# Moving the mask's count, the scales' signs and a block's statistics between engines in an attention and feed-forward kernel

## The chip, the cores and the metric

The kernel runs on one core of a Trainium2 chip. The metric is the device time of one execution in microseconds (us). The core's engines work side by side, each through its own list of instructions, in order: TensorE (PE in the profile; PEld are its weight loads), VectorE (DVE), ScalarE (ACT), GpSimd (POOL) and SyncE (SP), which here only issues transfers. An engine waits on another only through semaphores.

## The reference

`x` has 2048 rows of 256 numbers and `ctx` 1601 rows of 192. The result is `x` plus a cross attention, plus a feed-forward net with three weight matrices of signs. Cut to what matters here:

```python
n = layer_norm(layernorm(x)) ; q = n @ Wq ; k, v = split(ctx @ Wkv)      # 16 heads of 64
k = concat([null_k, k]) ; v = concat([null_v, v])                        # one null key: 1602 keys
sim = where(pad(mask, True), (q * 64**-.25) @ (k * 64**-.25).T, -max)    # mask: 1601 flags
x = x + layer_norm(softmax(sim) @ v @ Wout)
h = concat([n, -n]), n = layernorm(x)
h = relu(s0 * h @ W0) * 2 ; h = relu(s1 * h @ W1) * 2 ; h = s2 * h @ W2  # W = +1 or -1
x = x + h
```

`s0`, `s1` and `s2` are single numbers read from memory.

## The kernel before

**Units.** Heads go in pairs, 8 of them, and rows of `x` in blocks of 512, 4 of them. The main loop runs over 32 units (pair p, block b), unit u = 4p + b. In a unit, 13 tiles of 128 keys pass through scores (L414, `sT`), exponential (L440, `e`) and the weighted sum with the values (L447, `av`). Beside the scores TensorE computes the next unit's row maxima (L373, read by VectorE in L376). The tail of a unit combines the maxima (L381), turns them by a transpose (L386) and spreads them (L388, `mT`, read from the PSUM tile `mt`), projects the unit before out (L460), projects the queries of the unit after next (L215) and a half of the next pair's keys (L247, L252) or values (L316, L328).

**Order.** Everything stands in a hand-written order (`manual_schedule`): each engine issues its instructions as the code writes them, and a framework only adds the waits that the data needs.

**The denominators.** GpSimd adds the 13 exponentials into `acc`: tiles 1 and 2 (L689), 3 to 7 (L691), and then tile 0 and tiles 8 to 12 (L699). Tile 0 holds the last 66 keys, and before L699 may add it, and before TensorE may use it (it is the last group of L447), ScalarE scales its rows 64 and up by the column `spent` (L697). In the next unit ScalarE copies one number out of the finished `acc` (L680, `seen`) ahead of its exponential of tile 2, and so stands still there until the sums of the unit before are done.

**The mask's count.** Masked keys are set equal to the null key, and their number has to be taken out again. `masked_counted` (unit 0) reduces the mask's flags on VectorE (L400), subtracts 1601 (L401), puts the result in one row with a column of the identity (L402) and adds two more such columns (L404): the column `spent`.

**Input statistics.** Blocks 2 and 3 of `x` are normalised in units 0 and 1: `input_root` takes statistics on VectorE (L79, L80) and the root on ScalarE (L508, which loads a function table), `input_normed` takes a reciprocal (L512) and the negated mean (L142) on VectorE and eight row operations on ScalarE (L145, L146); then a one-number exponential (L712) loads ScalarE's other table again. `input_turned` in the tail of the same unit transposes the block (L525) and scales it into `xnT` (L526, L530), which the query projection L215 reads. In unit 1 the statistics already follow L381 on VectorE.

**The scales' signs.** In unit 3 VectorE computes `sgn` (sign of s0 and s1) and `s_out` (8 |s0| |s1| s2) from `s_sb` in five operations (L748 to L752), behind the masking of the second half of `ctx_b` (L407) and ahead of L388. `sgn` is first read in unit 28, `s_out` in the last layer.

**What lies on both sides of it.** GpSimd also does `keys_stepped` (L272) once for each pair. SyncE's transfers in this part (`ctx_b` a second time, the next pair's weights) are issued ahead of time.

Of the kernel before, what the change touches and what calls it, by code (L numbers as in the profile page):

```python
# [12 lines left out]
AF = mybir.ActivationFunctionType  # L13
ALU = mybir.AluOpType
# [5 lines left out]
M = 1601  # L20
# [8 lines left out]
KLAST = KEYS - 128 * (KC - 1)  # L29
# [9 lines left out]
def xattn_ffn(ctx, tc, x, ctxT, mask, g_norm, null_kv, wq, wkv, wout, g_out, k0, k1, k2, s0, s1, s2, out):  # L39
    nc = tc.nc  # L40
# [17 lines left out]
    s_sb = cp.tile([128, 3], F32, name="s_sb")  # L58
    sgn = cp.tile([128, 2], F32, name="sgn")
    s_out = cp.tile([128, 1], F32, name="s_out")  # L60
    eps_sb = cp.tile([128, 1], F32, name="eps_sb")
    eps2_sb = cp.tile([128, 1], F32, name="eps2_sb")
    ident = cp.tile([128, 128], F32, name="ident")
# [6 lines left out]
    warm = cp.tile([128, 1], F32, name="warm")  # L70

    def stats(src, n, name, mv=None):

        at = 0 if mv is None else 2
        if mv is None:
            mv = sp.tile([128, 4, 2], F32, tag="mv", name=f"mv_{name}")
        for j in range(n):
            st = sp.tile([128, 6], F32, tag="st", name=f"st_{name}_{at + j}")
            nc.vector.bn_stats(st, src[:, j, :])  # L79
            nc.vector.bn_aggr(mv[:, at + j, :], st)  # L80
        return mv
# [8 lines left out]
    def centred(dst, src, mv, r, j):  # L90
        nc.vector.tensor_scalar(dst, src, mv[:, j, 0:1], r[:, j : j + 1], ALU.subtract, ALU.mult)  # L91
# [47 lines left out]
    def centred_beside(dst, src, mv, r, b):  # L139

        nm = sp.tile([128, 4], F32, tag="nm", name=f"nm_{b}_{n_slots}")
        nc.vector.tensor_scalar(nm, mv[:, :, 0], -1.0, None, ALU.mult)  # L142
        for j in range(4):
            t = 4 * b + j
            nc.scalar.activation(dst[:, t, :], src[:, t, :], AF.Identity, bias=nm[:, j : j + 1])  # L145
            nc.scalar.mul(dst[:, t, :], dst[:, t, :], r[:, j : j + 1])  # L146

    with ExitStack() as att:
# [15 lines left out]
        spent = ap.tile([128, 1], F32, name="spent")  # L164
# [213 lines left out]
        def max_combined(p, b):  # L378

            cols = mcol.rearrange("p (j c) -> p c j", j=2)[:, 0:4, :]  # L380
            nc.vector.tensor_reduce(cols, maxima[p, b], AX.X, ALU.max, negate=True)  # L381
# [16 lines left out]
        def masked_counted():  # L398

            nc.vector.tensor_reduce(spent, keep[:, 1:], AX.X, ALU.add)  # L400
            nc.vector.tensor_scalar(spent, spent, float(M), None, ALU.subtract)  # L401
            nc.vector.tensor_tensor(spent, spent, ident[:, KLAST : KLAST + 1], ALU.mult)  # L402
            for row in range(64, KLAST):
                nc.vector.tensor_tensor(spent, spent, ident[:, row : row + 1], ALU.add)  # L404

        def context_masked(part, start, end):
            nc.vector.tensor_tensor(part[:, start:end], part[:, start:end], keep[:, start:end], ALU.mult)  # L407
# [97 lines left out]
        def input_root(b):  # L505
            mv = stats(x_sb[:, ts(b, 4), :], 4, f"x{b}")
            r = sp.tile([128, 4], F32, tag="rstd", name=f"rstd_x{b}")
            nc.scalar.activation(r, mv[:, :, 1], AF.Sqrt, bias=eps2_sb, scale=1.0 + EPS)  # L508
            return mv, r

        def input_normed(b, mv, r, beside=False):
            nc.vector.reciprocal(r, r)  # L512
            if beside:
                centred_beside(y_sb, x_sb, mv, r, b)
                return
            for j in range(4):
                centred(y_sb[:, 4 * b + j, :], x_sb[:, 4 * b + j, :], mv, r, j)
# [131 lines left out]
        with tc.manual_schedule():  # L649
            for u, (p, b) in enumerate(units):  # L650
# [40 lines left out]
                        nc.gpsimd.tensor_tensor(acc, acc, es[k], ALU.add)  # L691
                if nxt is not None:
                    max_combined(*nxt)
                if u == 0:
                    masked_counted()

# [7 lines left out]
                if u == len(units) - 2:  # L704
# [2 lines left out]
                    norm_end(0, y_sb, y_sb, beside=True)  # L707

                    nc.scalar.activation(warm, eps_sb, AF.Exp)
                if u < 2:  # L710
                    input_normed(u + 2, *input_root(u + 2), beside=True)
                    nc.scalar.activation(warm, eps_sb, AF.Exp)  # L712
                if u == 0:


                    nc.sync.dma_start(out=ctx_b[64:, 1:KEYS], in_=ctxT[128:CD, :])


# [24 lines left out]
                    context_masked(ctx_b, 0, 1024)  # L743
                if u == 3:
                    context_masked(ctx_b, 1024, KEYS)


                    nc.vector.tensor_scalar(sgn, s_sb[:, 0:2], 0.0, None, ALU.is_ge)  # L748
                    nc.vector.tensor_scalar(sgn, sgn, 2.0, -1.0, ALU.mult, ALU.add)
                    nc.vector.tensor_tensor(s_sb[:, 0:2], s_sb[:, 0:2], sgn, ALU.mult)  # L750
                    nc.vector.tensor_scalar(s_out, s_sb[:, 0:1], s_sb[:, 1:2], 8.0, ALU.mult, ALU.mult)
                    nc.vector.tensor_tensor(s_out, s_out, s_sb[:, 2:3], ALU.mult)  # L752
                if p + 1 < NP and b in (1, 2):
                    round_k(p + 1, b - 1)
                avs = lp.tile([128, 512], F32, tag="avs", name=f"avs_{p}_{b}", bufs=1)
# [172 lines left out]
```

## Time and profile before

| what | value |
|---|---|
| time, median of 3 runs | 1285.53 us (1283.4, 1285.53, 1285.76) |
| the profiled execution's own time | 1286.19 us |
| its span | 1284.4 us, granted TensorE clock 0.994 on average |
| unit 0: exponentials start | 38.65 us |
| unit 3: sums on GpSimd (L699) | start 162.32, take 15.27 us |
| unit 7: the same | start 300.59, take 14.90 us |
| feed-forward part | from 1098.69 us on |

The span is the profiled execution from its first to its last instruction; its own time has some 1.8 us more around it. "Busy" is the time in which an engine has an instruction in work. A line of the timeline gives the start, the time taken, the engine, the line of the kernel, the operation with output and input, and how long the engine had been idle before, with what released it. A line of a table by windows gives, for one stretch, the busy time of TensorE, its weight loads, VectorE, ScalarE and GpSimd with the number of instructions, then the granted TensorE clock (1.00 is full speed), and what the transfers did. The chain of work that ended last is followed back from the last instruction to whatever released each step.

### The profile page before, as it was taken

To read this page: it belongs to the slowest core of one execution; us is meant where nothing else is said; L and a number is where in the kernel's file an instruction comes from. 1 tells how busy PE (TensorE), PEld (TensorE's weight loads), DVE (VectorE), ACT (ScalarE), POOL (GpSimd) and SP (SyncE) were. 2 spreads that over 40 slices of the span, in tenths; PEclk is the share of its full clock that TensorE was granted. 3 is DMA by queue.
4 is the path that set the end of the run, shared out by engine and by line. 5 is a ranking of instruction groups with operands and counts; after the bars stand their busy time and mean duration, and the time that the engine had idled before them with its cause. 6 is when DMAs were issued, how large, how long until landed. Compare 5 with 4: busy or idle time off the path is not lost.

```text
span 1284.4 us, 19605 instructions
## 1 busy us (share of the span) xinstructions
PE 1264.9 (98%) x8336; PEld 651.5 (51%) x8336; DVE 768.3 (60%) x831; ACT 716.8 (56%) x974; POOL 1005.9 (78%) x505
## 2 busy tenths in 40 slices
PE   8999989999999999999999999999999999999998
PEld 6334444444444444444444444444444433788887
DVE  6778676656665666565666566656666783644432
ACT  3676645666566656666666666666666666422120
POOL 5688978899889988999889988998899999801100
PEclk9999989999999999999999999999999999999999
DMA  5100000000000000000000000000000010000000
GB/s 145 23 1 5 1 1 13 5 1 1 14 5 1 1 14 5 1 1 14 5 1 1 1 13 5 1 1 5 1 17 1 1 42 1 1 12 6 17 17 17
DMA packets 16169, 13.40 MB, mean 10 GB/s; under 512 B 2689, under 2 KB 15553, under 8 KB 16081
## 3 DMA queue, kind: packets, MB, share of 16 engines
q1 hardware_dynamic: 14944, 11.02, 3.1%
q8 instruction: 65, 1.06, 0.3%
q10 hardware_dynamic: 656, 0.79, 0.2%
q0 software_dynamic: 480, 0.34, 0.2%
q14 instruction: 24, 0.19, 0.0%
HBM read 10.04 MB, written 2.10 MB: 9 GB/s over the span
## 4 chain that ended last, share of the span: by engine, by line
PE 87%; POOL 7%; DVE 2%; ACT 2%; DMA 1%; issue 1%; SPq 0%; DVEq 0%; POOLq 0%; ACTq 0%
PE sT L414 26%; PE av L447 23%; PE ps L810 11%; PE max L373 6%; PE po L460 4%; PE psq L215 4%; POOL acc L699 4%; POOL acc L691 3%; PE ps L841 2%; PE psv L316 2%; PE psk L247 2%; PE psv L328 1%; PE sT L438 1%; PE den L471 1%; PE psk L252 1%; DMA x_sb<-in_x 1%
## 5 line engine op out<-in xcount | busy, mean ns | idle before, releaser
L376 DVE TENSOR_REDUCE mx<-max 128x2 f32<-128x1024 f32 x384 | 444.0, 1219 | 90.2 <-PE max L373 86.4
L699 POOL TENSOR_TENSOR acc<-acc,e 128x1024 f32<-128x1024 f32 x192 | 473.3, 2465 | 16.8 <-ACT e L697 1.8
L440 ACT ACTIVATE e<-sT 128x1024 f32<-128x1024 f32 x416 | 424.9, 1023 | 88.0 <-PE sT L438 45.3
L414 PE MATMUL sT<-qT,kT 64*128 64x512 f32 x1664 | 445.0, 609 | 5.1 <-ACT e L440 5.0
L691 POOL TENSOR_TENSOR acc<-acc,e 128x1024 f32<-128x1024 f32 x160 | 378.9, 2368 | 12.5
L447 PE MATMUL av<-e,v 128*32 128x512 f32 x3328 | 363.6, 592 | 0.0
L373 PE MATMUL max<-kr,qr 64*128 64x512 f32 x768 | 280.8, 719 | 0.8 <-DVE mx L376 0.8
L447 PEld LDWEIGHTS av<-e,v 128*32 128x32 f32 x3328 | 107.6, 110 | 237.5 <-issue 229.9
L414 PEld LDWEIGHTS sT<-qT,kT 64*128 64x128 f32 x1664 | 134.6, 186 | 135.8 <-ACT e L440 123.5
L689 POOL TENSOR_TENSOR acc<-e,e 128x1024 f32<-128x1024 f32 x32 | 75.6, 2361 | 76.5 <-ACT e L440 76.5
L373 PEld LDWEIGHTS max<-kr,qr 64*128 64x128 f32 x768 | 76.7, 188 | 88.9 <-DVE mx L376 66.2
L489 ACT COPY aoT<-r 32x256 f32<-32x256 f32 x224 | 90.2, 403 | 33.5 <-DVE r L483 31.2
L756 ACT COPY avs<-av 128x512 f32<-128x512 f32 x32 | 18.7, 585 | 145.0 <-PE av L447 145.0
L388 DVE TENSOR_TENSOR mT<-mt,pick 128x512 fp32r<-128x512 f32 x32 | 22.1, 691 | 116.9 <-PE mt L386 116.9
L490 DVE TENSOR_TENSOR aoT<-avs,aoT 128x512 f32<-128x512 f32 x28 | 26.9, 961 | 94.3 <-ACT aoT L489 94.3
L810 PE MATMUL ps<-h0hi,w 128*128 128x512 f32 x256 | 79.5, 392 | 0.0
L810 PE MATMUL ps<-h0lo,w 128*128 128x512 f32 x256 | 78.9, 390 | 0.0
L124 POOL TENSOR_TENSOR y_sb<-y_sb,gout_sb 128x256 f32<-128x256 f32 x12 | 9.3, 776 | 86.0 <-DVE y_sb L91 86.0
L216 ACT ACTIVATE qr<-psq 128x512 fp32r<-128x512 f32 x32 | 19.1, 597 | 95.0 <-PE psq L215 92.3
L798 ACT ACTIVATE h1hi<-ps 128x1024 fp32r<-128x1024 f32 x16 | 16.4, 1027 | 98.9 <-PE ps L810 98.9
L215 PE MATMUL psq<-xnT,wq 128*128 128x512 f32 x124 | 59.0, 599 | 2.0 <-ACT xnT L526 2.0
L460 PE MATMUL po<-wo,aoT 128*128 128x256 f32 x256 | 60.6, 380 | 0.0
(170 smaller groups left out, 1199.4 us busy)
## 6 DMA issues: line engine op xcount, KB each, us to landing
out_x<-o SPq DMA_DIRECT2D x7, 256.0 KB, 2.1
x_sb<-in_x SPq DMA_DIRECT2D x3, 512.0 KB, 9.1
wa<-in_wkv SPq DMA_DIRECT2D x8, 128.0 KB, 3.0
wq<-in_wq SPq DMA_DIRECT2D x8, 128.0 KB, 2.2
wo<-in_wout SPq DMA_DIRECT2D x8, 128.0 KB, 2.1
xnT<-in_k SPq DMA_DIRECT2D x1, 1024.0 KB, 5.5
wb<-in_wkv SPq DMA_DIRECT2D x15, 64.0 KB, 2.5
ctx_a<-in_ctxT SPq DMA_DIRECT2D x2, 256.0 KB, 7.3
```

The costliest lines, as they stand in the source:

```text
L215: nc.tensor.matmul(ps[:, 0, :], weights[p][0][:, c, :], xnT[:, b, c, :], start=c == 0, stop=c == 1)
L373: nc.tensor.matmul(ps[:, j, :w], qr[rows, ts(t, 128)], kr[rows, ds(start, w)], start=True, stop=True)
L376: nc.vector.tensor_reduce(maxima[p, b][:, t, :, c], ps[:, :, :w], AX.X, ALU.max)
L414: nc.tensor.matmul(ps[:n, j, :], kT[rows, ds(128 * KEY_TILES[k], n)], qT[rows, :], start=k < 2, stop=k >= 2, skip_group_check=k >= 2,)
L440: nc.scalar.activation(e, ps, AF.Exp)
L447: nc.tensor.matmul(av[ts(i, 32), 0, :], v[:n, KEY_TILES[k], ts(i, 32)], e[:n, i // 2, :], start=k == 1, stop=k == 0, tile_position=(0, 32 ...
L460: nc.tensor.matmul(pv[:, t, :], aoT[:, ts(t, 128)], weights[p][3], start=True, stop=True)
L489: nc.scalar.copy(aoT[ds(64 * j + 32 * rows, 32), ts(h, 256)], r[ds(64 * j + 32 * h, 32), :])
L689: nc.gpsimd.tensor_tensor(acc, es[1], es[2], ALU.add)
L691: nc.gpsimd.tensor_tensor(acc, acc, es[k], ALU.add)
L699: nc.gpsimd.tensor_tensor(acc, acc, es[k], ALU.add)
L810: nc.tensor.matmul(ps[:, f, :], w(c)[:, ts(2 * g + f, 128)], parts[part][:, c, :], start=i == 0, stop=i == len(steps) - 1,)
```

## The change

Three things are edited. In `masked_counted` the reduction of the mask stays on VectorE, and the small operations behind it go to GpSimd, the first two as one. The block that normalises blocks 2 and 3 of `x` (with its exponential of one number) is written ahead of the count and of the scaling by `spent`, instead of behind the sums of L699. The five operations on the scales go from VectorE in unit 3 to GpSimd in unit 4.

```diff
         def masked_counted():
 
             nc.vector.tensor_reduce(spent, keep[:, 1:], AX.X, ALU.add)
-            nc.vector.tensor_scalar(spent, spent, float(M), None, ALU.subtract)
-            nc.vector.tensor_tensor(spent, spent, ident[:, KLAST : KLAST + 1], ALU.mult)
+            nc.gpsimd.tensor_scalar(spent, spent, float(M), ident[:, KLAST : KLAST + 1], ALU.subtract, ALU.mult)
             for row in range(64, KLAST):
-                nc.vector.tensor_tensor(spent, spent, ident[:, row : row + 1], ALU.add)
+                nc.gpsimd.tensor_tensor(spent, spent, ident[:, row : row + 1], ALU.add)
...
                 if nxt is not None:
                     max_combined(*nxt)
+                if u < 2:
+                    input_normed(u + 2, *input_root(u + 2), beside=True)
+                    nc.scalar.activation(warm, eps_sb, AF.Exp)
                 if u == 0:
                     masked_counted()
 
                 nc.scalar.mul(es[0][64:], es[0][64:], spent[64:, 0:1])
                 for k in (0, *range(8, KC)):
                     nc.gpsimd.tensor_tensor(acc, acc, es[k], ALU.add)
...
-                if u < 2:
-                    input_normed(u + 2, *input_root(u + 2), beside=True)
-                    nc.scalar.activation(warm, eps_sb, AF.Exp)
                 if u == 0:
                     nc.sync.dma_start(out=ctx_b[64:, 1:KEYS], in_=ctxT[128:CD, :])
...
                 if u == 3:
                     context_masked(ctx_b, 1024, KEYS)
-                    nc.vector.tensor_scalar(sgn, s_sb[:, 0:2], 0.0, None, ALU.is_ge)
-                    nc.vector.tensor_scalar(sgn, sgn, 2.0, -1.0, ALU.mult, ALU.add)
-                    nc.vector.tensor_tensor(s_sb[:, 0:2], s_sb[:, 0:2], sgn, ALU.mult)
-                    nc.vector.tensor_scalar(s_out, s_sb[:, 0:1], s_sb[:, 1:2], 8.0, ALU.mult, ALU.mult)
-                    nc.vector.tensor_tensor(s_out, s_out, s_sb[:, 2:3], ALU.mult)
+                if u == 4:
+                    nc.gpsimd.tensor_scalar(sgn, s_sb[:, 0:2], 0.0, None, ALU.is_ge)
+                    nc.gpsimd.tensor_scalar(sgn, sgn, 2.0, -1.0, ALU.mult, ALU.add)
+                    nc.gpsimd.tensor_tensor(s_sb[:, 0:2], s_sb[:, 0:2], sgn, ALU.mult)
+                    nc.gpsimd.tensor_scalar(s_out, s_sb[:, 0:1], s_sb[:, 1:2], 8.0, ALU.mult, ALU.mult)
+                    nc.gpsimd.tensor_tensor(s_out, s_out, s_sb[:, 2:3], ALU.mult)
```

On VectorE the order in unit 0 becomes L381, statistics, reciprocal, negated mean, L400; on ScalarE, in units 0 and 1, the table load, the root, the eight row operations, the second table load and the exponential of one number stand ahead of L697. TensorE's and SyncE's instructions keep their order.

## The prediction

> **What bounds the kernel now.** I read the page's busy shares first, then the chain of work that ended last, then the timelines of ScalarE (ACT) and GpSimd (POOL) around the moved work, and last the granted clock by windows. "Unit" is one pass of the main loop (pair p, query block b, numbered 0 to 31); times are us from the span's start.
>
> ```profile
> PE 1264.9 (98%) x8336; PEld 651.5 (51%) x8336; DVE 768.3 (60%) x831; ACT 716.8 (56%) x974; POOL 1005.9 (78%) x505
> ...
> PE 87%; POOL 7%; DVE 2%; ACT 2%; DMA 1%; issue 1%; SPq 0%; DVEq 0%; POOLq 0%; ACTq 0%
> ```
>
> TensorE bounds nearly everything, so only places where it stands still can be won, or be made. The chain, in order of time, shows two such places where the edited lines stand; this is the one in unit 3:
>
> ```profile
> 163.17 2.00 issue
> 165.17 2.93 DVE ctx_b L407
> 168.10 2.25 DVE sgn L748
> 170.58 2.20 DVE s_sb L750
> 173.05 2.13 DVE s_out L752
> 175.18 0.61 DVE mT L388
> 175.84 2.50 PE psv L316 x10
> ```
>
> Columns are start, length, what. Three operations on two numbers take over 2 us each: each ends where a GpSimd sum ends. They hold L388, which frees the PSUM tile that L316 writes: the list of waits gives TensorE 3.9 us there. The other place is unit 0; first ScalarE, then GpSimd (start, length, engine, line, operation, idle before it and its releaser):
>
> ```profile
> 52.40 1.02 ACT L440 ACTIVATE e<-sT 128x1024 f32<-128x1024 f32 x1 [0.28 <-PE sT L414]
> 57.20 1.15 ACT L697 ACTIVATE e<-e,spent 64x1024 f32<-64x1024 f32 x1 [3.78 <-DVE spent L404]
> 58.37 1.28 ACT L508 ACT_TABLE_LOAD   x1
> ...
> 76.70 0.17 ACT L680 COPY seen<-acc 1x1 f32<-1x1 f32 x1
> ...
> 98.09 0.84 ACT L266 CAST kr<-kT 128x802 fp32r<-128x802 f32 x1
> ...
> 111.15 0.17 ACT L680 COPY seen<-acc 1x1 f32<-1x1 f32 x1
> ```
>
> ```profile
> 58.49 14.54 POOL L699 TENSOR_TENSOR acc<-acc,e 128x1024 f32<-128x1024 f32 x6 [1.79 <-ACT e L697]
> 77.97 2.37 POOL L689 TENSOR_TENSOR acc<-e,e 128x1024 f32<-128x1024 f32 x1 [4.94 <-ACT e L440]
> 80.41 12.16 POOL L691 TENSOR_TENSOR acc<-acc,e 128x1024 f32<-128x1024 f32 x5
> 92.65 16.40 POOL L699 TENSOR_TENSOR acc<-acc,e 128x1024 f32<-128x1024 f32 x6
> ```
>
> The reader is to see the coupling: the six sums of L699 start only after L697, and L680 in the next unit lets ScalarE go past k = 2 only when they are done. Unit 0's sums end at 73.03, and L680 comes at 76.70 (3.7 to spare); unit 1's end at 109.05 against 111.15 (2.1 to spare). Where nothing is spare the wait is real: the list of waits has
>
> ```profile
> ACT seen L680 <- POOL acc L699: 4.0, 3, 2.1
> ```
>
> (total us, times, longest; units 29 to 31). The windows show the clock falling behind both idle places:
>
> ```profile
> 70.00:72.00 2.00, 2.00 (x5) 0.83 (x3) 0.00 (x0) 1.14 (x3) 1.92 (x2) 0.50 0.00 0
> ...
> 176.00:178.00 2.00, 2.00 (x10) 2.00 (x10) 0.91 (x1) 0.00 (x0) 1.59 (x1) 0.50 0.00 0
> ```
>
> **Part 1, the signs leave unit 3 (gain).** Five VectorE operations go (2.31, 0.17, 2.19, 0.21, 2.13). L388 can then run when L407 ends (168.10) and its transpose is done (168.49), and L316 follows the query projection (170.06, 1.72 long as in unit 2) at 171.78 instead of 175.84. The price of stall and slow clock together comes from unit 7, the same block of the next pair, which has neither: from the copy L756 to L680 it takes 307.10 to 316.31 = 9.21; unit 3 takes 168.30 to 184.26 = 15.96. Gain 6.75. Its cover is thin: unit 3's sums end at 177.59, 9.29 behind L756, while L680 is now wanted at 9.21; unit 7's sums took 14.90 where unit 3's took 15.27, so I take no loss (0 to 0.4).
>
> The five operations on GpSimd stand behind unit 4's sums, where GpSimd idles 3.10 us before unit 5's first sum. The nearest row, 128x4 on GpSimd (L589), took 0.21: five are 1.05, hidden. Bounds: 0.14 (L587, 128x13) to 1.20 (L794, 128x1024 with pointer scalars), so 0.7 to 6.0; at 6.0 unit 5's sums are 2.9 late, 1.8 of it spare at unit 6's L680: up to 1.1 lost. The first reader of sgn is in unit 28.
>
> **Part 2, statistics ahead of the count, in units 0 and 1.** The diff moves the block not only past the count but past L697, and for `u < 2`. On ScalarE two table loads, the root, eight row operations and the warm-up (12 instructions) now stand ahead of L697; nothing of it is a DMA and the DMA queues keep their order.
>
> Unit 0. VectorE starts the statistics at 53.99, where the count was; in unit 1 they took 89.94 to 92.16 = 2.22, and the first operation behind the warm-up (L266) came 5.93 after that. So L697 starts at 53.99 + 2.22 + 5.93 = 62.14 and ends 63.29; with the same 0.14 to follow, the sums start at 63.43 (4.9 later) and end at 77.97. The count itself (1.81 from about 56.9) ends near 58.7, and three small GpSimd operations (0.6; 0.4 to 3.6) have 3.4 us until L697 is reached: nothing, at worst 0.2. TensorE's last group of L447 waits 0.35 for L697, and behind L697 stand L756 and L526, which wait for L447 and the transposes anyway. Then: L447 ends 64.2, transposes 1.09, scaled copy 0.75, projection at 66.1 instead of 67.43, at full clock (L215 1.72 and L247 1.35 as at 103.84 and 105.56, instead of 2.60 and 2.43: 1.96 less): the first scores of unit 1 come at 70.0 instead of 73.2. All of that is thrown away: L680 would be wanted 3.4 later, at 73.4 (in unit 2 it came at 111.15, the first scores at 107.78), and the sums end at 77.97. From L680 to the next scores took 1.16 (1041.41 to 1042.57, where L680 was waiting): 79.16 against 78.05 before. Loss 1.1.
>
> Unit 1 (times without that shift). L697 leaves 89.46 for the place of L266, 98.09; it ends 99.24, the sums start at 99.38 instead of 92.65. They take 14.54 rather than 16.40, since VectorE's two-input operations of 96.05 and 97.97 (2.00 and 4.00, stretched by waiting for GpSimd) are over. End 113.9 against 111.15 wanted; next scores 115.1 against 112.50. Loss 2.6. L447's last group (100.1) is not held.
>
> **The new idle time and the clock.** In unit 2 the scores behind L680 started 4.72 after the first ones (107.78 to 112.50), so in unit 1 TensorE could go on at 74.75 and stands still until 79.16, 4.4 us; in unit 2 2.6. Rows: 2.03 of idle in unit 0 was followed by half clock and cost 1.96; 3.90 in unit 3 cost 6.75 - 4.06 = 2.7; about 1.8 in unit 30 cost none (clock 1.00 from 1040 to 1044). So unit 1 pays 1.0 to 2.7, I take 1.9; unit 2 lies between the 1.8 without and the 2.03 and 3.90 with: 0 to 1.96, I take 1.0.
>
> The Trainium skill (TensorE: Matmul & The Clock Gate, "Why this matters for your kernels") speaks against this change: it asks for no idle gaps over about 3 us between bursts, since one window of idle halves the clock. By that rule unit 1 would pay and unit 2 not, and the sum would end 1.0 lower; the row of unit 0, slowed after 2.03, contradicts the rule's length, and I keep the rows.
>
> **Sum.** +1.1 + 2.6 - 6.75 + 1.9 + 1.0 = -0.15. The profiled execution took 1286.19 (span 1284.4 and 1.8 around it), so 1286.0; it lies 0.66 above the median of the runs, 1285.53, and carried to that the forecast is 1285.4. From unit 4 on both kernels issue the same work, and the shift travels unchanged.
>
> **Rivals** (times on the median).
> - The stalls cost no clock. -3.05: 1282.5, faster. For it: the 1.8 idle of unit 30; against: both longer idle places were slowed. 0.12.
> - L680 does not bite: unit 0's 3.2 and unit 3's 6.75 are both won, 1275.6. For it: it idles in 3 of 31 places only; against: the three show it bites as soon as the sums are late. 0.08.
> - GpSimd becomes the bound in units 3 and 4 (slower). With its sums 2.8 later and TensorE 6.75 earlier, unit 3's sums end after L680 is wanted. Decides from 9.21 us behind L756; before it was 9.29. If VectorE's two-input work stretches them as in unit 1 (16.40 for 14.90), ScalarE waits 1.5 in unit 4 and TensorE may pay a slow stretch of 1.96: -0.15 + 3.5, 1288.9. For it: the margin; against: unit 7. 0.25.
>
> **Chances.** The forecast has 0.55. 0.2% of the time, 2.6 us, is about what can be told from no change. Faster 0.20 (the first two rivals), same 0.55, slower 0.25 (the third). The unknowns make 1282.5 (no clock loss) to 1288.2 (-3.05 with 2.7, 1.96 and 1.1 for slow GpSimd operations on it) for the forecast; I reach up to 1288.9 to take in the third rival.
>
> **What would show it.** L697 in units 0 and 1 behind the warm-up, the sums starting near 63.4 and 100.5; L680 idle for some 4.6 us in unit 1 and 2.8 in unit 2 behind L699, a slow stretch after the first; no L748 to L752 on VectorE, L316 in unit 3 without idle ahead of it and clock 1.00; L680 in unit 4 with little or no idle. Wrong if L680 does not wait in units 1 and 2, if unit 3 keeps its stall, or if the slow stretches differ in number.

## The result and the profile after

The changed kernel takes 1286.74 us (median of 12 runs, 1283.97 to 1287.62), the kernel before 1283.74 us in the same comparison (12 runs, 1282.46 to 1285.76): a ratio of 1.0017 [1.0009, 1.0025], 3.0 us slower at the medians. The forecast was no change (-0.15). The time itself lies within the range, but the kernel moved, and upwards. The 1285.53 that the prediction started from was the median of three runs; over 12 runs the same kernel has 1.8 us less.

Every line behind the first edit has a new number, by one to four: L699 is now the scale by `spent` (L697 before), L701 the six sums behind it (L699), L679 the copy that waits for them (L680), L413 the scores, L439 the exponentials; L695, the exponential of one number, moved with its block (L712 before). The profiled execution took 1286.28, span 1284.5. Its busy shares, and the chain that ended last:

```profile
PE 1263.2 (98%) x8336; PEld 649.5 (51%) x8336; DVE 757.0 (59%) x822; ACT 717.3 (56%) x974; POOL 1006.2 (78%) x513
...
PE 86%; POOL 9%; ACT 2%; DMA 1%; DVE 1%; issue 1%; SPq 0%; DVEq 0%; POOLq 0%
```

VectorE lost 11 us of work (768.3 to 757.0), and GpSimd's share of the chain rose from 7% to 9%: the critical path now runs through the sums in two more places. ScalarE's and GpSimd's timelines (start, length, then idle before it and its releaser in brackets) show where:

```profile
63.06 0.20 ACT L695 ACTIVATE warm<-eps_sb 128x1 f32<-128x1 f32 x1
63.29 1.14 ACT L699 ACTIVATE e<-e,spent 64x1024 f32<-64x1024 f32 x1
...
79.08 0.19 ACT L679 COPY seen<-acc 1x1 f32<-1x1 f32 x1 [4.16 <-POOL acc L701]
...
102.01 1.14 ACT L699 ACTIVATE e<-e,spent 64x1024 f32<-64x1024 f32 x1
...
117.89 0.19 ACT L679 COPY seen<-acc 1x1 f32<-1x1 f32 x1 [2.81 <-POOL acc L701]
```

```profile
59.68 0.32 POOL L401 TENSOR_SCALAR spent<-spent,ident 128x1 f32<-128x1 f32 x1 [1.96 <-DVE spent L400]
60.08 0.46 POOL L403 TENSOR_TENSOR spent<-spent,ident 128x1 f32<-128x1 f32 x2
64.51 14.54 POOL L701 TENSOR_TENSOR acc<-acc,e 128x1024 f32<-128x1024 f32 x6 [3.96 <-ACT e L699]
...
103.30 14.56 POOL L701 TENSOR_TENSOR acc<-acc,e 128x1024 f32<-128x1024 f32 x6 [8.48 <-ACT e L699]
...
169.05 15.29 POOL L701 TENSOR_TENSOR acc<-acc,e 128x1024 f32<-128x1024 f32 x6
```

In units 0 and 1 the scale stands behind the exponential of one number, and the sums start when it is done: in unit 0 they take the same 14.5 us as before, in unit 1 14.56 where they took 16.40, but they start later. So L679 finds them unfinished in the next unit, for 4.16 and 2.81 us, where the kernel before had some to spare. The list of waits (total us, times, longest) has it as

```profile
ACT seen L679 <- POOL acc L701: 11.0, 5, 4.2
PE sT L413 <- ACT e L439: 11.5, 11, 3.9
```

against 4.0, 3 and 2.1 before for the first. The second line is the same wait one engine on: TensorE has filled its PSUM tiles with scores and stands 3.9 us until an exponential frees one. By windows (the granted clock is the third number from the end):

```profile
80.00:82.00 2.00, 1.76 (x6) 0.84 (x6) 0.00 (x0) 1.09 (x2) 1.73 (x1) 0.51 0.00 0
82.00:84.00 2.00, 2.00 (x10) 1.04 (x8) 1.21 (x1) 1.02 (x1) 1.92 (x2) 0.64 0.00 0
...
118.00:120.00 2.00, 0.95 (x6) 0.49 (x6) 0.00 (x0) 1.90 (x3) 0.93 (x1) 1.00 0.00 0
...
178.00:180.00 2.00, 2.00 (x17) 1.64 (x16) 0.12 (x1) 1.08 (x2) 1.92 (x2) 1.00 0.00 0
```

Half clock follows the wait in unit 1; in this execution none follows the one in unit 2, and unit 3 is at full speed. There the chain (start, length, what) has become all TensorE:

```profile
174.87 0.26 PE mt L386
175.13 1.73 PE po L459 x8
176.86 1.72 PE psq L215 x4
178.57 1.11 PE psv L316 x10
179.69 0.97 PE psv L328 x9
```

The 7.1 us that VectorE's operations on the scales took here before (168.10 to 175.18) are gone. To compare executions I cut each span at the first exponential of units 0 to 5. The first column is the start-up, the last all that follows unit 4; us, one execution each.

| kernel (experiments below) | start-up | unit 0 | unit 1 | unit 2 | unit 3 | unit 4 | rest |
|---|---|---|---|---|---|---|---|
| before, profile of the prediction | 38.65 | 35.87 | 34.44 | 33.52 | 39.59 | 32.86 | 1069.5 |
| before, repeated | 37.70 | 35.75 | 34.45 | 33.51 | 38.62 | 32.86 | 1069.5 |
| after | 39.69 | 32.89 | 40.21 | 36.33 | 32.85 | 32.91 | 1069.6 |
| after, repeated | 38.39 | 32.88 | 40.02 | 36.31 | 32.85 | 32.90 | 1069.6 |
| signs alone | 36.91 | 35.83 | 34.45 | 33.51 | 32.85 | 32.86 | 1069.5 |
| statistics and count alone | 37.35 | 32.86 | 41.30 | 37.87 | 38.07 | 32.86 | 1069.5 |
| after, unit 1's block put back | 38.87 | 32.88 | 40.17 | 33.51 | 32.85 | 32.87 | 1069.6 |
| after, filled in units 1 and 2 | 37.39 | 32.88 | 38.66 | 36.34 | 32.84 | 32.92 | 1069.7 |
| after, filled in unit 1 | 37.22 | 32.87 | 38.63 | 37.91 | 32.85 | 32.86 | 1069.7 |
| after, filled in unit 2 | 37.48 | 32.88 | 40.27 | 36.30 | 32.84 | 32.89 | 1069.6 |
| before, filled in unit 0 | 37.45 | 34.14 | 34.45 | 33.51 | 38.67 | 32.86 | 1069.6 |
| after, L679 at k = 7 everywhere | 36.89 | 32.88 | 34.56 | 33.70 | 32.97 | 32.97 | 1070.2 |
| after, L679 at k = 7 in units 1 and 2 | 37.76 | 32.86 | 34.57 | 33.70 | 32.85 | 34.35 | 1069.6 |
| signs, count in the start-up | 38.09 | 32.31 | 34.44 | 33.53 | 32.85 | 32.86 | 1069.6 |

The table is the key to all that follows: where an edit does not touch a unit, the unit repeats within some 0.1 (unit 3 with its stall apart), and what varies between executions of one kernel is the start-up and whole steps of some 1.5 us in a unit where TensorE stood.

### The profile page after: what moved, and what is told of

It reads as the page before. It is cut to its first block, busy times and chain, and to the rows that moved or that the text cites. A ratio compares the mean times of both kernels' runs of the same rounds, so it can differ in the third digit from the quotient of the medians.

```text
span 1284.5 us, 19600 instructions
## 1 busy us (share of the span) xinstructions
PE 1263.2 (98%) x8336; PEld 649.5 (51%) x8336; DVE 757.0 (59%) x822; ACT 717.3 (56%) x974; POOL 1006.2 (78%) x513
## 3 DMA queue, kind: packets, MB, share of 16 engines
q8 instruction: 65, 1.06, 0.3%
## 4 chain that ended last, share of the span: by engine, by line
PE 86%; POOL 9%; ACT 2%; DMA 1%; DVE 1%; issue 1%; SPq 0%; DVEq 0%; POOLq 0%
PE sT L413 25%; PE av L446 23%; PE ps L806 11%; PE max L373 6%; POOL acc L701 6%; PE po L459 4%; PE psq L215 3%; POOL acc L690 3%; PE ps L837 2%; PE psv L316 2%; PE psk L247 1%; PE den L470 1%; PE psv L328 1%; PE sT L437 1%; DMA x_sb<-in_x 1%; ACT e L439 1%
## 5 line engine op out<-in xcount | busy, mean ns | idle before, releaser
L701 POOL TENSOR_TENSOR acc<-acc,e 128x1024 f32<-128x1024 f32 x192 | 471.3, 2455 | 27.3 <-ACT e L699 12.4
L439 ACT ACTIVATE e<-sT 128x1024 f32<-128x1024 f32 x416 | 424.9, 1024 | 88.0 <-PE sT L437 43.4
L413 PE MATMUL sT<-qT,kT 64*128 64x512 f32 x1664 | 445.7, 609 | 11.5 <-ACT e L439 11.5
L413 PEld LDWEIGHTS sT<-qT,kT 64*128 64x128 f32 x1664 | 134.9, 186 | 143.0 <-ACT e L439 129.7
L795 DVE SCALAR_TENSOR_TENSOR h1lo<-ps,h1hi 128x1024 fp32r<-128x1024 f32 x16 | 19.6, 1224 | 67.7 <-ACT h1hi L794 67.7
```

The lines of the kernel that those rows point to most:

```text
L413: nc.tensor.matmul(ps[:n, j, :], kT[rows, ds(128 * KEY_TILES[k], n)], qT[rows, :], start=k < 2, stop=k >= 2, skip_group_check=k >= 2,)
L439: nc.scalar.activation(e, ps, AF.Exp)
```

## The experiments

The kernels ran in three series, and each is compared with the kernel before in its own series, which had a median of 1283.94 (21 runs) in the first, 1283.92 (29) in the second and 1284.54 (21) in the third. Ratios are given with their 95% interval.

**The kernel before, unchanged.** No edit.

> The kernel before, unchanged, for the granted clock of each of its executions. Theory: the idle 2.03 us of unit 0 is followed by a slow stretch in some executions only, so that the times fall into two groups some 2 us apart, 1283 and 1285.6, and the slower group has the lower mean clock (0.994 against about 0.997). Rival: the two groups come from the transfers at the start; then the mean clock is the same in both.

1284.01 (11 runs), ratio 1.0003 [0.9994, 1.0011]. Its runs sort by clock: 0.998 at 1282.31 and 1282.76, 0.997 from 1283.43 to 1284.88, 0.996 at 1285.56 and 1285.84. So the spread of some 3 us among runs of one kernel goes with how long the clock was halved, though not in the two groups expected. Nor is unit 0 what varies: all three profiles that keep its idle 2.03 us have the slow stretch behind it, and the two profiles of this kernel differ in the start-up and in unit 3. In unit 3 this profile, by windows, has

```profile
174.00:176.00 2.00, 1.23 (x8) 1.23 (x9) 1.85 (x3) 0.00 (x0) 1.92 (x2) 0.87 0.00 0
176.00:178.00 2.00, 2.00 (x11) 1.77 (x11) 0.00 (x0) 0.00 (x0) 0.53 (x1) 0.50 0.00 0
178.00:180.00 2.00, 2.00 (x12) 1.68 (x13) 0.00 (x0) 0.88 (x2) 0.00 (x0) 0.77 0.00 0
```

where the profile that the prediction was made from has

```profile
174.00:176.00 2.00, 0.17 (x1) 0.17 (x2) 2.00 (x3) 0.00 (x0) 1.92 (x2) 0.62 0.00 0
176.00:178.00 2.00, 2.00 (x10) 2.00 (x10) 0.91 (x1) 0.00 (x0) 1.59 (x1) 0.50 0.00 0
178.00:180.00 2.00, 2.00 (x13) 1.78 (x14) 0.00 (x0) 0.00 (x0) 0.00 (x0) 0.50 0.00 0
180.00:182.00 2.00, 2.00 (x11) 1.62 (x11) 0.00 (x0) 0.88 (x2) 0.00 (x0) 0.67 0.00 0
```

What the clock took away, summed as (1 - clock) times 2 us, is 1.72 in the first and 3.42 in the second: one stretch against two in a row. Unit 3 takes 38.62 against 39.59. The execution that gave the prediction its price had a doubled one; of the other 13 profiles one has that too, in unit 1 (statistics and count alone).

**The signs alone.** The third edit of the change and nothing else:

```diff
                 if u == 3:
                     context_masked(ctx_b, 1024, KEYS)
-                    nc.vector.tensor_scalar(sgn, s_sb[:, 0:2], 0.0, None, ALU.is_ge)
...
+                if u == 4:
+                    nc.gpsimd.tensor_scalar(sgn, s_sb[:, 0:2], 0.0, None, ALU.is_ge)
...
```

> The five operations on the scales go to GpSimd in unit 4, all else as before. Theory: the whole gain of unit 3, 6.75 us, so about 1277.0 against a median before of 1283.74; L316 without idle ahead of it, clock 1.00 there. Rival (GpSimd becomes the bound): L680 of unit 4 waits 1.5 us or more and TensorE slows down, 1279 to 1280.

1278.23 (5 runs), ratio 0.9959 [0.9947, 0.9972]: -5.7, not -6.75. By the table the edit acts in unit 3 and nowhere else, 38.62 to 32.85 = -5.8. Of the four profiles that keep the stall, unit 3 took 38.07, 38.62, 38.67 and 39.59; the gain is 5.2 to 6.7 by the execution one looks at. In the kernel before, the three slow operations ended within 0.03 us of a GpSimd sum (170.34, 172.76 and 175.18 against 170.31, 172.75 and 175.16) though the list of waits has no wait of VectorE for GpSimd there; what couples them is not shown.

**Statistics and count alone.** The first two edits, with the signs left on VectorE:

```diff
-            nc.vector.tensor_scalar(spent, spent, float(M), None, ALU.subtract)
-            nc.vector.tensor_tensor(spent, spent, ident[:, KLAST : KLAST + 1], ALU.mult)
+            nc.gpsimd.tensor_scalar(spent, spent, float(M), ident[:, KLAST : KLAST + 1], ALU.subtract, ALU.mult)
...
+                if u < 2:
+                    input_normed(u + 2, *input_root(u + 2), beside=True)
+                    nc.scalar.activation(warm, eps_sb, AF.Exp)
                 if u == 0:
                     masked_counted()
...
-                if u < 2:
-                    input_normed(u + 2, *input_root(u + 2), beside=True)
-                    nc.scalar.activation(warm, eps_sb, AF.Exp)
```

> The count's small operations go to GpSimd and the statistics' block stands ahead of the scaling by spent, as in the changed kernel; the signs stay on VectorE in unit 3. Theory: 1.1 and 2.6 of waiting, two slow stretches, and the 2 us that a before without a slow stretch in unit 0 does not have to lose: 1291.5 to 1294, that is the changed kernel plus 6.75. Rival (the late sums cost little, and the changed kernel merely lacks the gain of unit 3): 1284 to 1287.

1291.58 (5 runs), ratio 1.0057 [1.0044, 1.0070]: +7.6, just inside the expected range, where the prediction's terms for this part make +6.6. With the signs' -5.7 it makes +1.9, inside the interval of the whole change (0.0009 to 0.0025 of 1284, 1.2 to 3.2): the parts add, as far as the runs can tell.

**Unit 1's block put back.** The kernel after, with the block moved in unit 0 alone:

```diff
-                if u < 2:
+                if u == 0:
                     input_normed(u + 2, *input_root(u + 2), beside=True)
                     nc.scalar.activation(warm, eps_sb, AF.Exp)
...
+                if u == 1:
+                    input_normed(u + 2, *input_root(u + 2), beside=True)
+                    nc.scalar.activation(warm, eps_sb, AF.Exp)
                 if u == 0:
                     nc.sync.dma_start(out=ctx_b[64:, 1:KEYS], in_=ctxT[128:CD, :])
```

> The changed kernel, but in unit 1 the statistics' block stands behind the sums again; only unit 0 has it ahead of the scaling. Theory: L680 of unit 2 no longer waits, 2.6 us less, and with it goes the slow stretch behind that wait in most executions, up to 1.7 more: 1282.4 to 1284.1. L680 of unit 1 still waits some 4 us. Rival (only unit 0's wait matters): 1286.7 as the changed kernel.

1281.48 (11 runs), ratio 0.9981 [0.9972, 0.9990], 0.9 below the expected range. Unit 2 is back at 33.51, its wait gone: moving the block in unit 1, where no count is in the way, was pure loss, and without it the change would have been a gain.

**The kernel after, unchanged.** No edit.

> The kernel after, unchanged, for a second profile. Cut at the first exponential of units 0 to 5, the span of the first profile was 39.69, 32.89, 40.21, 36.33, 32.85, 32.91 and 1069.6; that of the kernel before (its repeat) 37.70, 35.75, 34.45, 33.51, 38.62, 32.86 and 1069.5. Theory A (the 3 us of the result are stretches at half clock, and the start-up differs by chance from one execution to the next): the first number comes anywhere from 36.9 to 39.7, units 0, 3, 4 and the rest repeat within 0.1, and only units 1 and 2 move, by whole slow stretches (some 1.5 to 2 each); median 1285.5 to 1287.6. Theory B (the changed program starts up later): the first number is 39.5 or more again.

1285.98 (11 runs), ratio 1.0014 [1.0006, 1.0023]: slower again, by 2.1. Units 0 to 4 repeat within 0.2. The start-up came at 38.39, so theory B's bound of 39.5 is not met; but both profiles of this kernel have a slow stretch in the start-up (around 20 to 26 us), as only two of the other twelve have. Theory A's numbers all hold. A stretch in the start-up is not bound to the changed program: seven of the 12 runs of the next kernel, whose start-up is the same, have no slow stretch at all. Whether it comes more often in the kernel after, the runs do not tell.

**Filling TensorE's idle time.** Matmuls whose output nobody reads stand where TensorE waits behind L679 (four in unit 1, two in unit 2); the wait itself stays. In both units:

```diff
                         max_chunk(*nxt, order[k])
+                        if k == 3 and u in (1, 2):
+                            busy = flex(f"busy_{u}")
+                            for _ in range(4 if u == 1 else 2):
+                                nc.tensor.matmul(busy[:, 0, :], ident, xnT[:, 0, 0, :], start=True, stop=True)
```

> The kernel after with matmuls added that nobody reads, in units 1 and 2, where TensorE waits for the copy behind GpSimd's sums (four 128x512 in unit 1, two in unit 2). The wait itself stays. Theory (besides the wait, its slow clock is paid): no stretch at half clock behind the wait in unit 1, 1.9 less there, and 0 to 1.7 less in unit 2: median 1283.1 to 1284.8, unit 1 at 38.3 where it was 40.2. Rival (the clock has no share, or is paid elsewhere): 1286.7 or, with matmuls that do not fit into the wait, up to 1288.7.

1282.72 (12 runs), ratio 0.9990 [0.9981, 0.9998]: faster than before by 1.2, and than the kernel after by 3.3 (2.06 + 1.20), with more work on TensorE; 0.4 below the expected range. L679 waits the same 4.15 and 2.81. This execution is 2.3 us earlier than that of the kernel after. By windows the clock behind the wait in unit 1 is whole, where it was 0.51 and 0.64:

```profile
78.00:80.00 2.00, 2.00 (x12) 0.99 (x12) 0.68 (x1) 1.68 (x2) 2.00 (x1) 1.00 0.00 0
80.00:82.00 2.00, 2.00 (x16) 1.00 (x12) 2.00 (x3) 1.80 (x3) 1.92 (x2) 1.00 0.00 0
```

Seven of the 12 runs, 1281.90 to 1282.88, had a granted clock of 1.000 throughout, which no run of the kernel after had. Then in one unit at a time, with `u == 1` and `u == 2` in the condition:

> The added matmuls in unit 1 alone. With them in both units the median was 1282.7, 3.3 to 4.0 under the kernel after; the profiles showed 1.4 to 1.6 of that in unit 1 and nothing in unit 2. Theory (executions of the kernel after mostly have a slow stretch in unit 2 as well, which its two profiles happen to miss, at 1.5 as in the kernel with the second part alone): median 1283.8 to 1284.6, the share of runs with a granted clock of 1.000 falls. Rival (unit 2's wait costs no clock): 1282.7 as with both.

> The added matmuls in unit 2 alone. Unit 1 takes 40.0 to 40.2 with its slow stretch, unit 2 36.3. Theory (stretches of some 1.5 in unit 1 always and in unit 2 mostly, which add up): median 1284.1 to 1284.7. Rival (unit 2's wait costs no clock): no less than the kernel after, 1286.0 to 1286.7.

Unit 1 alone: 1283.72 (11 runs), ratio 0.9994 [0.9985, 1.0002]; unit 2 alone: 1284.80 (11 runs), ratio 1.0002 [0.9993, 1.0011]; each is 0.1 outside its expected range. Against the kernel before of each series the kernel after, those filled in unit 1, in unit 2 and in both stand at +2.06, -0.82, +0.26 and -1.20, so unit 1's fill saves 2.9 or 1.5 (without and with the other), unit 2's 1.8 or 0.4. Each of the four has an uncertainty of about 1, so for unit 2 the times alone do not settle it. The profile of the kernel filled in unit 1 does: it caught the stretch that the two profiles of the kernel after missed in unit 2:

```profile
114.00:116.00 2.00, 1.04 (x6) 0.49 (x6) 0.00 (x0) 1.81 (x2) 1.02 (x1) 0.93 0.00 0
116.00:118.00 2.00, 2.00 (x10) 1.04 (x6) 1.21 (x1) 1.02 (x1) 1.92 (x2) 0.50 0.00 0
118.00:120.00 2.00, 2.00 (x11) 1.08 (x8) 1.09 (x2) 1.05 (x2) 1.92 (x2) 0.72 0.00 0
```

Unit 2 takes 37.91 there and 36.30 to 36.34 without it: 1.6 for a stretch. In unit 1 it is 40.02 to 40.27 against 38.66 and 38.63, 1.4 to 1.6.

**The same in the kernel before, unit 0.** Two matmuls behind the transpose L386:

```diff
             nc.tensor.transpose(ps[:, 0, :128], mcol, ident)
+            if (p, b) == (0, 1):
+                for _ in range(2):
+                    nc.tensor.matmul(ps[:, 1, :], ident, xnT[:, 0, 0, :], start=True, stop=True)
```

> The kernel before with two matmuls added that nobody reads, in unit 0 behind the maxima's transpose, where TensorE stood for 2.03 us. Theory (that idle halves the clock behind it at a price of 1.96): unit 0, from its first exponential to that of unit 1, takes 33.8 where it took 35.75 to 35.87 in the three profiles that have it, the clock there reads 1.00, median 1281.9. Rival (the slow stretch has another cause): unit 0 stays at 35.8 and the median at 1283.9.

1282.52 (11 runs), ratio 0.9990 [0.9982, 0.9999]. Unit 0 takes 34.14, 1.6 to 1.7 less, and the clock reads 1.00 there; in the kernel before (its repeat) these windows are

```profile
66.00:68.00 2.00, 1.52 (x2) 0.84 (x3) 0.00 (x0) 0.43 (x1) 1.92 (x2) 0.57 0.04 8
68.00:70.00 2.00, 2.00 (x4) 0.80 (x3) 0.00 (x0) 0.00 (x0) 1.92 (x2) 0.58 0.00 0
```

The mechanism holds, the price of 1.96 was some 0.3 too high, and the median kept 0.6 above the expected 1281.9: two groups of runs remain, 1282.2 to 1282.5 and 1283.6 to 1284.0, with clocks of 0.998 and 0.997. The profiled run, of the first group, has one stretch, in unit 3; where the second group has its other one is not shown.

**L679 moved to k = 7.** The kernel after with the gate later in the unit:

```diff
-                    if k == 2 and last is not None:
+                    if k == 7 and last is not None:
                         nc.scalar.copy(seen[:, 1:2], last[3][:1, 0, 0:1])
```

> The kernel after with ScalarE's copy that waits for GpSimd's last sum moved from k = 2 to k = 7 of the next unit. Theory (that copy's place is what makes late sums cost time): unit 1 takes 34.5 where it took 40.2, unit 2 33.5 where it took 36.3 to 37.9, units 29 to 31 lose part of their 4.0 us of waits; median 1273 to 1278. Rival (another reader of the sums, or GpSimd's own load, sets the pace): the wait moves to the next reader and the median stays within 2 us of 1286.7.

1276.58 (5 runs), ratio 0.9940 [0.9928, 0.9951]. Units 1 and 2 take 34.56 and 33.70. ScalarE's timeline in unit 1 (start, length):

```profile
71.09 6.63 ACT L439 ACTIVATE e<-sT 128x1024 f32<-128x1024 f32 x6 [0.30 <-PE sT L437]
77.62 0.17 ACT L679 COPY seen<-acc 1x1 f32<-1x1 f32 x1
```

Six exponentials pass ahead of L679, most of them while the sums run on, and L679 then finds the sums done (they ended at 76.26, 61.70 + 14.56). So the sums being late costs nothing in itself; the place of the copy makes it cost. The waits of units 29 to 31 vanish too, but the rest did not get shorter, it took 0.6 more: that part of the expectation missed. A version with the late place in units 1 and 2 alone (`7 if u in (1, 2) else 2`) was to win the 0.6 back:

> The kernel after with the copy at k = 7 in units 1 and 2 alone, at k = 2 elsewhere. With k = 7 everywhere, units 0 to 4 took 32.88, 34.56, 33.70, 32.97 and 32.97, and the rest 1070.23 where the kernel after has 1069.6. Theory (the late place is needed only where the sums are late, and costs a little elsewhere): the rest at 1069.6, units 3 and 4 at 32.9, median 1275.8 to 1276.1. Rival (the rest was long by chance): 1276.6.

1277.19 (5 runs), ratio 0.9944 [0.9932, 0.9957]: the rest is at 1069.6 again, but unit 4 lost 1.5, and the median is above both expectations. ScalarE and GpSimd there:

```profile
175.56 0.19 ACT L679 COPY seen<-acc 1x1 f32<-1x1 f32 x1 [1.55 <-POOL acc L701]
```

```profile
141.12 3.94 POOL L272 TENSOR_TENSOR kT<-kT 128x256 f32<-128x256 f32 x5
...
160.24 15.29 POOL L701 TENSOR_TENSOR acc<-acc,e 128x1024 f32<-128x1024 f32 x6
```

GpSimd carried its lateness through unit 2, added the key steps of L272, and came to unit 4 late. A wait taken away in units 1 and 2 was met again in unit 4.

**The count in the start-up.** The kernel before with the signs on GpSimd, the count moved ahead of the main loop with its small operations on GpSimd, and the statistics where the kernel before has them:

```diff
         project_q(0, 0, slot)
+        masked_counted()
...
                 if nxt is not None:
                     max_combined(*nxt)
-                if u == 0:
-                    masked_counted()
```

> The signs on GpSimd, and the count of the mask in the prologue with its small operations on GpSimd; the statistics stay where the kernel before has them. The scale of unit 0 then waits for nothing, and the sums start some 3.7 earlier instead of 4.9 later. Theory: unit 0 takes 32.9 without a slow stretch, units 1 to 4 as with the signs alone (34.45, 33.51, 32.85, 32.86), no wait behind the sums; median 1275.3, or up to 1277.2 if the count's 1.81 delays the prologue. Rival (unit 0's gain needs the statistics ahead of the scale): unit 0 at 35.8, median 1278.2 or more.

1275.53 (5 runs), ratio 0.9931 [0.9918, 0.9943]: some 9 us less than the kernel before, and the lowest median of all that ran, though its interval overlaps that of L679 at k = 7. ScalarE, then GpSimd, in unit 0:

```profile
52.88 1.15 ACT L695 ACTIVATE e<-e,spent 64x1024 f32<-64x1024 f32 x1
...
72.58 0.17 ACT L680 COPY seen<-acc 1x1 f32<-1x1 f32 x1
```

```profile
56.21 14.61 POOL L697 TENSOR_TENSOR acc<-acc,e 128x1024 f32<-128x1024 f32 x6
```

The scale (here L695) follows the last exponential without a wait, the sums run through and end at 70.82, and the copy (here L680) finds them done with 1.8 to spare. Unit 0 takes 32.31: the gain of the statistics' early start comes without the price, since what held both up was the count.

## Why the prediction was wrong, point by point

- **Which waits, and how long: right.** L699 was to start near 62.14 in unit 0 and did at 63.29 in an execution whose main loop began 1.04 later; L679 was to idle 4.6 and 2.8 and idled 4.16 and 2.81. Without the clock's share the two cost +1.3 (32.88 + 38.66 of the filled kernel against 35.75 + 34.45) and +2.8 (36.33 - 33.51); +1.1 and +2.6 were predicted.
- **Small GpSimd operations: right.** 0.78 for the count's three (0.6 predicted), hidden, since GpSimd then stands 3.96 until L699 is through; the signs' five ran from 215.21 to 216.64, hidden too.
- **The clock: right in kind.** Predicted 1.9 + 1.0 = 2.9; the fills together saved 3.3, give or take about 1. A stretch costs 1.4 to 1.6; unit 1 has one in all five profiles with its wait unfilled, unit 2 in two of four.
- **The step that failed: "Gain 6.75" in unit 3.** It measured 5.7 by the medians and 5.8 by the repeated profile. The step set the profiled unit 3 against unit 7, and the profiled execution had two slow stretches there where the others had one: of the same 3.9 us stall in the same place, one execution paid 1.0 more than another. This alone is 1.0 of the error, and it was read as if it were the edit's.
- **The other terms were each small by 0.2 to 0.4, all in the same direction.** Nothing was there to cancel them: +1.3 + 2.8 + 3.3 - 5.8 = +1.6, where the prediction's terms made -0.15. Measured were +3.0 and +2.1 by the medians; the intervals of the ratios are 1.2 to 3.2 and 0.8 to 3.0.
- **The carrying to a median** has the same flaw: the sum stood on an execution with four slow stretches (clock 0.994), and on a median of three runs, 1285.53, that later runs put at 1283.7 to 1284.5. It shifts the forecast time up by 1.0 to 1.8, not the forecast change; that the time still came out within 1.4 of the forecast is luck, since this and the missed change have opposite signs.
- **The rivals.** That the stalls cost no clock fell (0.51 in the window behind unit 1's). That L679 does not bite fell. GpSimd as the bound in unit 4 came to its threshold and stopped there: the sums ended at 184.34, L679 came at 184.36, and unit 4 takes 32.91 for 32.86.

What stays open is 0.5 to 1.4 us between the sum of the measured terms and the two medians, inside the intervals. Eight of the changed kernel's 12 runs have a granted clock of 0.996, which is three stretches (3 x 1.7 of 1284 us), where its two profiles have two, one of them in the start-up; which place the third is in, the runs do not tell.

## What to carry to other kernels

Follow a step that you move to every engine it passes: here a block of ScalarE's work, put ahead of a scale that GpSimd's sums wait for, cost more than the VectorE work it was put ahead of. When a gain is read as one profiled stretch against a clean one, find out first how much of the stretch varies from execution to execution (several profiles of the unchanged kernel, cut at the same marks), and take only what repeats as the edit's. And where small work holds up two consumers, take it out of the way altogether before reordering them.

## What the hardware did that was not expected

The slow clock came in steps, not in proportion to the idle time ahead of it. Summed as (1 - clock) times the window's 2 us, the stretch took 1.70 in unit 1 of the kernel after, 1.70 in unit 2 of the kernel filled in unit 1, 1.72 in unit 3 of the repeated kernel before, and twice that, 3.42, in the first profile's unit 3: half clock for some 3.4 us, or for two such pieces. Part of it can fall on time in which TensorE stands anyway and costs nothing, which is why the price in a unit varied: in the first profile's unit 3 TensorE stood for 1.36 us of the doubled stretch.

Whether an idle time is followed by one looks like chance: 2.03 us in unit 0 was in all three profiles that have it, 3.9 us in unit 1 in five of five, 2.5 us in unit 2 in two of four, and the idle times of 0.6 to 0.8 us in the start-up in four of fourteen. The traces' clock records show more. In each of the 14 profiles every change of the clock lies a whole number of windows of 3.41 us from every other, and where these windows lie differs from execution to execution. Here is the same gap of 2.5 us in unit 2 cut at them, in the kernel after (two lines) and in the kernel filled in unit 1 (two lines); TensorE's busy time stands behind the window's length:

```profile
114.15:117.56 3.41, 2.35 (x14) 0.81 (x10) 3.30 (x4) 0.93 (x1) 3.33 (x2) 1.00 0.00 0
117.57:120.98 3.41, 1.93 (x12) 1.08 (x12) 0.75 (x2) 2.77 (x4) 2.19 (x2) 1.00 0.00 0
112.31:115.72 3.41, 0.87 (x8) 0.49 (x6) 1.40 (x2) 1.92 (x3) 2.20 (x2) 1.00 0.00 0
115.73:119.14 3.41, 3.41 (x12) 1.73 (x10) 1.44 (x2) 1.74 (x3) 3.33 (x2) 0.50 0.00 0
```

Split into 1.06 and 1.48 us the gap cost no clock; 2.54 us in one window were followed by a window at half clock. Behind the start-up this holds throughout the 14 profiles: all 14 windows at full clock with 2.00 us of idle or more were followed by one at half clock, and none with 1.81 or less. The doubled stretch fits: in the first profile's unit 3 the 3.9 us fell as 2.54 and 1.36, the second part already at half clock, and another slow window followed; in the repeated one they fell as 1.22 and 2.69, and one followed. So the extra 1.0 in the prediction's price came from where the gap lay. The start-up does not separate as cleanly (1.39 to 1.64 us of idle followed by half clock in four profiles, up to 1.40 not in the other ten), and stays open.

The Trainium skill (TensorE: Matmul & The Clock Gate, "Why this matters for your kernels") asks for no idle gaps over about 3 us; here gaps of 2.0 and 2.5 us were followed by half clock, and the measurement decides. With matmuls whose output nobody reads there was no stretch in any of the five places where they were profiled, and in unit 0 of the kernel before they alone were worth 1.4 us.
